# LSH attention and ternary feed-forward: a coarse column shift inside the score matmul, coefficients on GpSimd, two rounded passes for the ternary layers

## The chip, the core and the metric

The kernel runs on one core of a Trainium2 chip. The engines are TensorE (PE, with its weight loads PEld), VectorE (DVE), ScalarE (ACT), GpSimd (POOL) and the queue of SyncE (SP), which issues nearly all transfers. The metric is the device time of one execution in microseconds. Before the change it is 1344.95 us, the median of 3 runs (1344.68 to 1345.1).

## The reference

One layer on x of 16 images x 512 tokens x 128 features. First an attention of 16 heads with 8 features each, whose scores are q against q itself, then a feed-forward part with ternary weights; both read a layer norm of x and add a layer norm of their result to x.

```python
q = (x @ Wq.T + bq).reshape(B, S, H, Dh)
v = (x @ Wv.T + bv).reshape(B, S, H, Dh)
qa = jnp.concatenate([q, jnp.ones((B, S, H, 1), q.dtype)], axis=-1)
bits = (jnp.einsum('bshe,en->bshn', qa, hyperplanes) >= 0).astype(jnp.int32)
buckets = jnp.einsum('bshn,n->bsh', bits, 2 ** jnp.arange(NH, dtype=jnp.int32))
...
scores = jnp.einsum('bhsd,bhtd->bhst', q, q) / jnp.sqrt(jnp.float32(E))
same = (b_hs[:, :, :, None] == b_hs[:, :, None, :]).astype(scores.dtype)
coeff = NB - 2 + same                       # 62, or 63 in the same bucket of 64
attn = jax.nn.softmax(scores * coeff, axis=-1)
out = jnp.einsum('bhst,bhtd->bhsd', attn, v)
...
h = jax.nn.silu(_tlin(x, w1_w, w1_s)) * _tlin(x, w2_w, w2_s)     # 128 -> 512
h = jax.nn.gelu(_tlin(h, h1_w, h1_s), approximate=False)         # 512 -> 512
h = jax.nn.gelu(_tlin(h, h2_w, h2_s), approximate=False)         # 512 -> 512
return _tlin(h, w3_w, w3_s)                                      # 512 -> 128
```

`_tlin(x, w, s)` is x times the transposed w, scaled by s for each output; the entries of w are -1, 0 or 1.

## The kernel before, in words

The program is one long straight list of instructions for each engine. A small planner, the class `Order`, decides the order of that list while the program is built: every piece of work is a generator that asks for buffers from a `Pool`, waits on an `Event`, and yields one operation with an engine, a cost and a rank; the planner runs all generators against a simulated clock and emits an operation when its engine is free there. So the order on each engine is fixed before the program runs, and each engine works through it strictly in that order.

Index j counts the 256 heads of all images (j = 16 b + h), each with 4 tiles of 128 x 512.

- `prep(b)`, L605 to L807, makes q for image b, splits it into three bf16 parts (`qparts`), writes each part twice to memory (L651, L652), and makes the bucket numbers, once as rows (`bkd`) and once as columns (`bj`). `inputs()`, L533 to L600, finds mean and variance of x for the images after the first with accumulating activations on ScalarE.
- `gather(j)`, L812 to L853, fetches the parts of one head as two operands of 72 rows (9 products of parts, 8 features each) and the bucket row on 128 partitions. All three transfers go through SP.
- `scores()`, L872, makes one tile of scores in PSUM by one bf16 matmul. `coeffs()`, L890, makes the tile of coefficients 62 or 63 on VectorE. `logits()`, L925, multiplies both on VectorE and in the same instruction keeps the maximum of each row (the tile is symmetric, so the maximum of a row is that of a column too).
- `maxima()`, L958 and L963, turns the maxima of two heads and writes them to memory; `softmax()`, L975, reads them back as a row on all partitions (`mb`), subtracts that row from the four tiles on GpSimd in one instruction of 128 x 2048 (L982) and exponentiates on ScalarE (L987). Five heads (`BY_ROWS`) go another way, with the maximum as a bias.
- `attend(gg)`, L1048, multiplies the weights of four heads with v, four matmuls side by side in the array, with a column of ones that gives the denominators; L1069 turns the result, L1079 and L1080 divide.
- `residual`, `added` and `ffn(b)` follow for each image: gate products L1200 with w1 and w2, silu on ScalarE L1188, their product on VectorE L1170, two hidden layers L1244 with gelu L1258, the last layer L1282, norm and output. All these matmuls are float32. The last image runs in two halves. `weights()` loads the weights and folds scales and means into them.
- `activity()`, L1419, keeps TensorE busy with matmuls of zeros until the first feed-forward block starts.

Buffers that the change touches: 11 tiles of logits, 3 banks of PSUM for scores, 3 for the feed-forward part and 2 for the rest, 4 sets of gathered rows, 4 tiles of coefficients.

Of the kernel before, what the change touches and what calls it, by code (L numbers as in the profile page):

```python
# [14 lines left out]
BF16 = mybir.dt.bfloat16  # L15
AF = mybir.ActivationFunctionType
# [5 lines left out]
P = 128  # L22
EPS = 1e-5
NBKT = 64

# [165 lines left out]
def tile_lsh_attention_ffn(  # L191
    ctx: ExitStack,
    tc: tile.TileContext,
    x: bass.AP,
# [30 lines left out]
    KS = NP * NP * DH  # L225
    BR, BC, BP = 3, 172, 174
# [9 lines left out]
    LB = 11  # L236
    BY_ROWS = (3, 7, 11, 15, 19)
    SLOTS = H * NT
    N = B * SLOTS

# [39 lines left out]

    junk = const.tile([P, E], BF16, name="junk")
# [7 lines left out]

    block = const.tile([E, H], F32, name="block")  # L290
    nc.vector.reduce_sum(
        block, ident.rearrange("r (h d) -> r h d", d=DH), axis=AX.X
    )
    hp_sb = const.tile([E, H, NH], F32, name="hp_sb")
# [68 lines left out]
    score_banks = Pool("s", 3)  # L363
    ffn_banks = Pool("f", 3)
    banks = Pool("b", 2)
    logit_bufs = Pool("l", LB)
    row_bufs = Pool("r", 4)
    co_bufs = Pool("co", 4)
    mx_bufs = Pool("mx", 2)
    mb_bufs = Pool("mb", 3)  # L370
    row_mx_bufs = Pool("rx", 2)
    h_bufs = Pool("h", 3)
    x1_bufs = Pool("x1_", 2)
    xnt_bufs = Pool("xntf", 1)
    avs_bufs = Pool("avs", 1)
    a_bufs = Pool("a", 2)

    NB_ = B * NG
    gathered, exped = events(B * H), events(B * H)
    scored, weighed = events(N), events(N)  # L380
# [116 lines left out]
    def turned(xn, xnt, k, tp, tiles):  # L497

        cols = slice(tiles[0] * P, (tiles[-1] + 1) * P)

        def turn():
            for t in tiles:
                nc.tensor.transpose(tp[:, ts(t, P)], xn[:, t, :], ident)

        yield pe(0.125 * len(tiles), 2, turn)
        yield act(0.13 + 0.0925 * len(tiles), -2, lambda: nc.scalar.copy(xnt[:, cols], tp[:, cols]))
        od.put(banks, k)
# [21 lines left out]
    rs_x = const.tile([P, B, NT], F32, name="rs_x")  # L529
    nm_x = const.tile([P, B, NT], F32, name="nm_x")  # L530
    known = events(B)

    def inputs():  # L533
        for b0, b1 in zip(GROUPS, GROUPS[1:]):
            n = b1 - b0
            sums = const.tile([P, 2, n, NT], F32, name=f"sx_{b0}")
            ve = const.tile([P, n, NT], F32, name=f"vx_{b0}")
            late = 6 if b0 == 1 else LATE
            if b0 > 1:
                yield wait(gathered[1])  # L540
            for b in range(b0, b1):
                xt = p2.tile([P, NT, E], F32, tag="xtm", name=f"xtm_{b}", bufs=1)
                yield dma(
                    256,
                    2,
                    lambda: nc.sync.dma_start(
                        out=xt, in_=x[b].rearrange("(p t) e -> p t e", t=NT)
                    ),
                )

                def sum_(ts_):
                    for t in ts_:
                        nc.scalar.activation(
                            junk,
                            xt[:, t, :],
                            AF.Identity,
                            scale=ROOT / E,
                            accum_out=sums[:, 0, b - b0, t : t + 1],
                        )

                def square(ts_):
                    for t in ts_:
                        nc.scalar.activation(
                            junk,
                            xt[:, t, :],
                            AF.Square,
                            scale=-ROOT,
                            bias=sums[:, 0, b - b0, t : t + 1],
                            accum_out=sums[:, 1, b - b0, t : t + 1],
                        )  # L570

                yield act(1.0, late, lambda: sum_((0, 1)))
                yield act(1.0, late, lambda: sum_((2, 3)))
                yield act(1.2, late, lambda: square((0, 1)))
                yield act(1.2, late, lambda: square((2, 3)))
            yield act(
                0.22,
                -5,
                lambda: nc.scalar.activation(ve, sums[:, 1], AF.Identity, bias=eps),
            )  # L580
            yield pool(
                1.0,
                0,
                lambda: nc.gpsimd.tensor_tensor(
                    rs_x[:, b0:b1], ve, mhalf[:, 0:n], op=ALU.pow
                ),
            )
            k = yield get(banks)
            mp = bank(k, f"mp_{b0}")[:, 0 : n * NT].rearrange("p (b t) -> p b t", t=NT)
            yield act(0.22, -5, lambda: nc.scalar.copy(mp, sums[:, 0]))  # L590
            yield dve(
                0.1,
                1,
                lambda: nc.vector.scalar_tensor_tensor(
                    nm_x[:, b0:b1], mp, -(float(E) ** 0.5), rs_x[:, b0:b1], op0=ALU.mult, op1=ALU.mult
                ),
            )
            od.put(banks, k)
            for b in range(b0, b1):
                od.set(known[b])  # L600


    qds, bkds, bjs = {}, {}, {}

    def prep(b):  # L605
# [14 lines left out]
        if b:  # L620
            yield wait(known[b])
            xn = p2.tile([P, NT, E], F32, tag="xna", name=f"xn_a{b}", bufs=1)
            xnt = p1.tile([P, S], F32, tag="xnta", name=f"xnt_a{b}")
            yield from rescale(xt, lambda t: xn[:, t, :], (nm_x[:, b], rs_x[:, b]), ALL)
            k = yield get(banks)
            yield from turned(xn, xnt, k, bank(k, f"tp_a{b}"), ALL)
        else:
            xnt = p1.tile([P, S], F32, tag="xnta", name=f"xnt_a{b}")
            yield from norm_transposed(xt, xnt, f"a{b}", 1, ALL)
# [13 lines left out]
        qd = [  # L643
            dram.tile([H, DH, NP, S], BF16, tag="qd0", name=f"qd0_{b}"),
            dram.tile([H, NP, DH, S], BF16, tag="qd1", name=f"qd1_{b}"),
        ]
        kept = events(NP)

        def keep(i):
            def emit():  # L650
                nc.sync.dma_start(out=qd[0][:, :, i, :], in_=qparts[i])  # L651
                nc.sync.dma_start(out=qd[1][:, i, :, :], in_=qparts[i])  # L652

            yield dma(256, 1, emit, cost=0.7)
            od.set(kept[i])
# [97 lines left out]
        od.spawn(keep(0))  # L753
        yield wait(read)
# [57 lines left out]
    def gather(j, tag):  # L812
        b, h = divmod(j, H)
        yield wait(prepared[b])
        ql = p1.tile([KS, S], BF16, tag=f"ql{tag}", name=f"ql_{j}")
        qr = p1.tile([KS, S], BF16, tag=f"qr{tag}", name=f"qr_{j}")
        bb = p1.tile([P, BR * BP], BF16, tag=f"bb{tag}", name=f"bb_{j}")
        rows[j] = (ql, qr, bb, tag)

        yield dma(  # L820
            74,
            1 + j * 1e-3,
            lambda: nc.sync.dma_start(
                out=ql,
                in_=qds[b][1][h]
                .rearrange("i d s -> (i d) s")
                .unsqueeze(1)
                .to_broadcast([NP * DH, NP, S]),
            ),
            held=False,  # L830
# [658 lines left out]
```

## Time and profile before

| | |
|---|---|
| median of 3 runs | 1344.95 us |
| span of the profiled execution | 1343.1 us, granted TensorE clock 0.987 |
| transfers | 174.03 MB, mean 130 GB/s, 45.7% of 16 engines for the main queue |
| DVE L925, 1024 logit tiles with their maxima | 663.0 us busy, mean 678 ns |
| DVE L890, 1024 coefficient tiles | 450.1 us busy, mean 470 ns |
| ACT L987, 251 exponentials of a whole head | 478.2 us busy, mean 1908 ns |
| PE L1244, hidden layers, 1088 records for 544 matmuls | 495.5 us busy |
| PE L872, 1024 score matmuls | 346.6 us busy, mean 383 ns |
| PE L1048, weights times v, 2048 records for 1024 matmuls | 270.3 us busy |
| ACT table loads, 178 in all | 1283 ns each |

A group's line gives source line, engine, operation, output and inputs with their shapes, the count, then busy time and the mean duration of one, then the idle time just before these instructions and what ended it. Durations of neighbours overlap on an engine, since an instruction starts before the one in front of it has drained; so the groups' busy times add up to more than the engine's busy time, and the distance between two starts is the better price in a full queue. A float32 matmul shows as two records. In the timelines the columns are start, duration, engine, line, operation, tiles and count; in the table of stretches each engine's busy time and count are followed by the granted clock, the share of the transfer engines and their rate.

### The profile page before, as it was taken

Reading aid. Unit: us, or ns where it says so; the run is one execution under the profiler, and the core shown is the slowest. Engines: PE = TensorE matmul, PEld = TensorE weight load, DVE = VectorE, ACT = ScalarE, POOL = GpSimd, SP = SyncE. Lnnn points to the kernel's source line nnn. Section 1 sums busy time; section 2 is a strip of 40 time slices with the busy share of each in tenths; the row PEclk is TensorE's granted clock in tenths of the full one; section 3 lists DMA queues with packets and bytes.
Section 4 is the critical chain, followed back from the end, with each engine's and each line's share of the span. In section 5 each row is a group of like instructions: output and inputs, shape, how many; then the busy total and the mean of one; then the engine's idle time right before and its main releaser. Section 6 shows DMA issues by size and latency. Waiting matters only on the chain.

```text
span 1343.1 us, 21064 instructions
## 1 busy us (share of the span) xinstructions
PE 1293.6 (96%) x6009; PEld 577.7 (43%) x6009; DVE 1220.4 (91%) x3867; ACT 1119.6 (83%) x1560; POOL 1196.7 (89%) x316
## 2 busy tenths in 40 slices
PE   8999999998999999999999999999999999999897
PEld 3444344344443343444334344434444344434367
DVE  5999999999999899999999999999999999999220
ACT  3688888889998897988888788888989798888953
POOL 1497999999999999999999999999999999999810
PEclk9999999998999999999999999999999999999999
DMA  4755455455544445455544545454545545444100
GB/s 132 198 142 149 128 156 134 139 144 146 148 142 116 129 141 145 133 141 137 149 123 122 146 132 155 123 143 120 149 129 142 138 139 140 131 120 119 48 9 8
DMA packets 158865, 174.03 MB, mean 130 GB/s; under 512 B 33821, under 2 KB 117277, under 8 KB 158749
## 3 DMA queue, kind: packets, MB, share of 16 engines
q1 hardware_dynamic: 155937, 169.20, 45.7%
q10 hardware_dynamic: 2811, 3.48, 0.9%
q8 instruction: 48, 0.79, 0.2%
q14 instruction: 69, 0.56, 0.2%
HBM read 153.50 MB, written 19.13 MB: 129 GB/s over the span
## 4 chain that ended last, share of the span: by engine, by line
PE 55%; DVE 25%; DMA 7%; POOL 5%; issue 5%; ACT 3%; SPq 1%; POOLq 0%; ACTq 0%; DVEq 0%
PE hp L1244 23%; PE av L1048 12%; DVE l L925 12%; PE sp L872 10%; DVE co L890 9%; POOL l L982 5%; PE w L1200 4%; DMA mb<-md 4%; PE yp L1282 2%; PE op L1069 1%; DMA bb<-bkd 1%; DVE h L1170 1%; DMA ql<-qd 1%; ACT l L987 1%; PE pp L674 1%
## 5 line engine op out<-in xcount | busy, mean ns | idle before, releaser
L982 POOL TENSOR_TENSOR l<-l,mb 128x2048 f32<-128x2048 f32 x251 | 1134.9, 4553 | 39.8 <-DMA mb<-md 33.1
L925 DVE CUSTOM_DVE_ANT_0 l<-co,sp 128x512 f32<-128x512 bf16 x1024 | 663.0, 678 | 14.9 <-PE sp L872 10.0
L987 ACT ACTIVATE l<-l 128x2048 f32<-128x2048 f32 x251 | 478.2, 1908 | 38.9 <-POOL l L982 33.9
L1244 PE MATMUL hp<-h,h 128*128 128x512 f32 (+1 forms) x1088 | 495.5, 569 | 0.4 <-ACT h L1258 0.4
L890 DVE TENSOR_SCALAR co<-bb,bj 128x516 bf16<-128x516 bf16 x1024 | 450.1, 470 | 1.1 <-DMA bb<-bkd 0.7
L872 PE MATMUL sp<-qr,ql 72*128 72x512 bf16 x1024 | 346.6, 383 | 33.8 <-DVE mxpad L925 30.3
L1244 PEld LDWEIGHTS hp<-h,h 128*128 128x128 f32 x1088 | 202.0, 190 | 159.4 <-issue 134.7
L1048 PE MATMUL av<-l,vaug 128*32 128x512 f32 x2008 | 251.4, 607 | 0.0
L872 PEld LDWEIGHTS <-ql 72*128 72x128 bf16 x1024 | 91.2, 98 | 279.0 <-issue 258.4
L1200 PE MATMUL w<-xnt_f,w 128*128 128x512 f32 (+1 forms) x272 | 133.6, 591 | 4.4 <-ACT a L1188 4.2
L1048 PEld LDWEIGHTS av<-l,vaug 128*32 128x32 f32 x2008 | 55.1, 110 | 146.6 <-issue 123.2
L987 ACT ACT_TABLE_LOAD x87 | 111.6, 1283 | 1.5
L1419 PE MATMUL activity<-still 128*128 128x512 bf16 x325 | 89.5, 387 | 1.0 <-DVE still L283 1.0
L925 DVE DVE_READ_ACCUMULATOR2_ANT mxpad<- 128x1 f32 x1004 | 81.6, 81 | 0.0
L1258 ACT ACT_TABLE_LOAD x59 | 75.7, 1283 | 0.9
L1200 PEld LDWEIGHTS w<-xnt_f,w 128*128 128x128 f32 x272 | 51.5, 197 | 49.0 <-issue 23.8
L1062 ACT COPY avs<-av 128x512 f32<-128x512 f32 x64 | 37.0, 578 | 41.8 <-PE av L1048 41.6
L1170 DVE TENSOR_TENSOR h<-w,a 128x512 f32<-128x512 f32 (+1 forms) x68 | 44.1, 652 | 30.0 <-PE w L1200 19.6
L1282 PEld LDWEIGHTS yp<-w,h 128*128 128x128 f32 x512 | 65.4, 191 | 13.0 <-issue 9.0
L1282 PE MATMUL yp<-w,h 128*128 128x128 f32 x512 | 65.9, 275 | 0.0
L457 POOL TENSOR_TENSOR rs_y<-ve_y,mhalf 128x4 f32<-128x4 f32 (+1 forms) x17 | 16.5, 969 | 50.3 <-ACT ve_y L446 50.1
L1258 ACT ACTIVATE h<-hp,h1s 128x512 f32<-128x512 f32 (+1 forms) x68 | 42.0, 660 | 14.3 <-PE hp L1244 13.9
(105 smaller groups left out, 954.6 us busy)
## 6 DMA issues: line engine op xcount, KB each, us to landing
mb<-md SPq DMA_DIRECT2D x251, 256.0 KB
bb<-bkd SPq DMA_DIRECT2D x256, 130.5 KB
ql<-qd SPq DMA_DIRECT2D x256, 72.0 KB
qr<-qd SPq DMA_DIRECT2D x255, 72.0 KB
qd<-q SPq DMA_DIRECT2D x96, 128.0 KB
xta<-in_L_attn_x_dram SPq DMA_DIRECT2D x16, 256.0 KB
xtr<-in_L_attn_x_dram SPq DMA_DIRECT2D x16, 256.0 KB
xtm<-in_L_attn_x_dram SPq DMA_DIRECT2D x15, 256.0 KB
```

The lines of the kernel that those rows point to most:

```text
L872: nc.tensor.matmul(sp, lhsT=ql[:, ts(t, P)], rhs=qr, start=True, stop=True)
L890: nc.vector.tensor_scalar(co, bb.rearrange("p (r c) -> p r c", c=BP)[:, :, 0:BC], bjs[b][:, c : c + 1], float(NBKT - 2), op0=ALU.is_equal, ...
L925: nc.vector.tensor_tensor_reduce(out=l, in0=co[:, 0:S], in1=sp, scale=1.0, scalar=-3.0e38, op0=ALU.mult, op1=ALU.max, accum_out=mx[:, t : ...
L982: lambda: nc.gpsimd.tensor_tensor(l, l, mb.unsqueeze(1).to_broadcast([P, NT, S]), op=ALU.subtract),
L987: yield act(1.82, 0, lambda: nc.scalar.activation(l, l, AF.Exp, scale=SCALE), "exp")
L1048: nc.tensor.matmul(av[k * Q : (k + 1) * Q, :], lhsT=va[:, t, c : c + Q], rhs=ls[gg * GH + k][0][:, t, :], start=(t == 0), stop=(t == NT - 1),)
L1170: lambda: nc.vector.tensor_tensor(h[:, c, cols], g2, a, op=ALU.mult),
L1200: lambda: nc.tensor.matmul(gp, lhsT=w_sb[which][:, 0, ts(c, P)], rhs=xnt[:, cols], start=True, stop=True),
L1244: lambda i=i: nc.tensor.matmul(hp, lhsT=w[:, i, ts(c, P)], rhs=hin[:, i, cols], start=(i == 0), stop=(i == NC - 1),),
L1258: nc.scalar.activation(h[:, c, cols], hp, AF.Gelu, scale=sc[:, c : c + 1])
L1282: nc.tensor.matmul(yp[:, ts(t, E)], lhsT=h[:, i, ts(t, P)], rhs=w_sb["w3"][:, i, :], start=(i == 0), stop=(i == NC - 1),)
L1419: nc.tensor.matmul(bk, lhsT=still, rhs=still.unsqueeze(1).to_broadcast([P, NT, P]), start=start, stop=stop,)
```

## The change

- **The shift inside the score matmul.** For images 1 to 15 the maximum of a column is no longer found. Instead each query gets a level, its own squared length in steps, rounded and capped (`levels`). 64 rows are added to the score matmul's 64 rows of q: on one side the one-hot code of the bucket, on the other that code less 63, times the level (`code`). In the same bucket they add -62 x level, in another -63 x level; times the coefficient 63 or 62 both give the same number, so a whole column is shifted by a constant, which the softmax takes out again. One part product is dropped there (8 instead of 9). Exponentials then follow at once, with a fixed bias of -25 (`weights_of`). Image 0 keeps the old way, its subtraction cut in two.
- **q in memory** is now one chain of 10 slots for each head, of which an operand is slots 0 to 8 or 1 to 9, so that both operands come in one transfer (`qlr`).
- **Coefficients** of images 1 to 15 are made on GpSimd, and so is the one-hot code of each pair of heads; the second half of the code is made on VectorE, and SP writes it into the operand.
- **Two passes.** The inputs of w1, w2, h1 and h2 are split into a value rounded to float32r and the rest, and go through TensorE in two float32r passes; w3 stays float32. For the hidden layers GpSimd makes both (`split`). The scales no longer go into the weights, so the feed-forward norm subtracts its mean again.
- **silu** becomes tanh, times and plus on VectorE, with the scales in the product.
- **Moments of x** are taken in `prep` on VectorE; `inputs()` is gone.
- **A guard.** The new body notes whether all denominators lay within limits and whether all weights were unchanged by the rounding; at the end a branch on that number (`doubt`) runs the old form of the body in full if they did not.
- **Buffers.** 7 tiles of logits, 5 banks of PSUM shared by all but the scores, 6 sets of rows, 2 tiles of coefficients for image 0 and 6 for GpSimd's, 2 for codes of pairs, 2 for split halves.

```diff
+    CHAIN = (2, 2, 1, 1, 0, 1, 2, 0, 0, 2)
+    KS = (len(CHAIN) - 1) * DH
...
-        yield dma(74, ..., ql)
-        yield dma(74, ..., qr)
+                out=qlr[0:n],
+                in_=bass.AP(tensor=chain.tensor, offset=chain.offset + first * S,
+                    ap=[[S, n], [DH * S, 2], [1, S]]),
...
+        if b in running:
+            yield wait(coded[j])
+            code, i, kp, left = codes.pop(j)
+            yield dma(128, 1 + j * 1e-3,
+                lambda: nc.sync.dma_start(
+                    out=qlr[NBKT:P], in_=code[i * NBKT : (i + 1) * NBKT]), cost=0.43)
...
-                    nc.vector.tensor_scalar(
+                    (nc.gpsimd if pooled else nc.vector).tensor_scalar(
                         co,
                         bb.rearrange("p (r c) -> p r c", c=BP)[:, :, 0:BC],
                         bjs[b][:, c : c + 1],
                         float(NBKT - 2),
                         op0=ALU.is_equal,
                         op1=ALU.add,
                     )
...
+                    if mx is None:
+                        nc.vector.tensor_tensor(l[:, t, :], co, sp, op=ALU.mult)
+                        return
...
+    def weights_of(j, l):
+        yield act(1.82, 0, lambda: nc.scalar.activation(
+            l, l, AF.Exp, bias=base, scale=SCALE), "exp")
+        od.set(exped[j])
...
+    def levels(b, square):
+        yield pe(0.3, 2, lambda: nc.tensor.matmul(rowp, lhsT=own, rhs=square, start=True, stop=True))
+        yield dve(0.6, 2, lambda: nc.vector.tensor_scalar(
+            rowp, rowp, LEVELS, WHOLE, op0=ALU.min, op1=ALU.add))
+        yield dve(0.6, 2, lambda: nc.vector.tensor_scalar(
+            level, rowp, -WHOLE, UNIT, op0=ALU.add, op1=ALU.mult))
...
+    def code(b, h, kp):
+        yield dma(132, ..., pb, in_=bkds[b][two].unsqueeze(1).to_broadcast([2, NBKT, BR * BP]))
+        yield dma(128, ..., pz, in_=zds[b][two].unsqueeze(1).to_broadcast([2, NBKT, S]))
+        yield pool(0.55, RHOT, mark)            # hot[:, 0] = (pb == number)
+        yield dve(0.6, RCODE, lambda: nc.vector.scalar_tensor_tensor(
+            hot[:, 1, :], hot[:, 0, :], 1.0 - NBKT, pz, op0=ALU.add, op1=ALU.mult))
...
+                nc.scalar.activation(a, gp, AF.Tanh, scale=w_sb["w1sh"][:, c : c + 1])
+                nc.vector.scalar_tensor_tensor(a, a, 1.0, gp, op0=ALU.add, op1=ALU.mult)
...
+                nc.vector.scalar_tensor_tensor(
+                    h[:, c, cols], g2, w_sb["gs"][:, c : c + 1], a, op0=ALU.mult, op1=ALU.mult)
...
+        def split(layer, hin, khin, before):
+                    yield pool(..., nc.gpsimd.tensor_copy(hi[:, :, cols], hin[:, two, cols]))
+                yield pool(..., nc.gpsimd.tensor_tensor(
+                    lo[:, :, cols], hin[:, two, cols], hi[:, :, cols].bitcast(F32), op=ALU.subtract))
...
+                for k, r in enumerate(rs):
+                    nc.tensor.matmul(hp, lhsT=w[:, i, ts(c, P)], rhs=r,
+                        start=(i == 0 and k == 0), stop=(i == NC - 1 and k == len(rs) - 1))
...
+def tile_lsh_attention_ffn(tc, *args):
+    with tc.tile_pool(name="verdict", bufs=1) as kept:
+        doubt = kept.tile([1, 1], I32, name="doubt")
+        body(tc, doubt, *args)
+        v = nc.values_load(doubt, min_val=0, max_val=2**20)
+    with tc.If(v > 0):
+        body(tc, None, *args)
```

## The prediction

> **What bounds the kernel now.** I read the page's busy shares first, then the stretches, the groups and the timelines of single engines.
>
> ```profile
> span 1343.1 us, 21064 instructions
> PE 1293.6 (96%) x6009; PEld 577.7 (43%) x6009; DVE 1220.4 (91%) x3867; ACT 1119.6 (83%) x1560; POOL 1196.7 (89%) x316
> ```
>
> ```profile
> core 0: us, PE busy (x) PEld busy (x) DVE busy (x) ACT busy (x) POOL busy (x), PEclk, DMA share, GB/s
> 0.00:60.00 60.00, 56.07 (x250) 25.92 (x251) 43.38 (x141) 27.75 (x73) 19.01 (x15) 1.00 0.56 157
> 60.00:600.00 540.00, 520.18 (x2469) 224.20 (x2468) 525.51 (x1660) 476.35 (x726) 513.34 (x127) 0.98 0.51 141
> 600.00:1240.00 640.00, 625.79 (x2887) 269.19 (x2889) 631.53 (x2004) 554.95 (x649) 629.00 (x161) 0.99 0.49 135
> 1247.00:1343.10 96.10, 84.86 (x374) 54.87 (x374) 13.08 (x43) 55.35 (x102) 28.39 (x13) 0.97 0.06 20
> ```
>
> From 60 to 1240 us VectorE and GpSimd both stand at 97 to 98%: two full engines in one ring. The last 96 us belong to the last feed-forward blocks on TensorE. The groups say what fills them:
>
> ```profile
> L982 POOL TENSOR_TENSOR l<-l,mb 128x2048 f32<-128x2048 f32 x251 | 1134.9, 4553 | 39.8 <-DMA mb<-md 33.1 <-DVE co L890 5.2 <-DVE mxpad L925 1.5
> ...
> L1362 POOL TENSOR_TENSOR w<-w,scale 128x512 f32<-128x512 f32 x2 | 2.5, 1268 | 15.3 <-DMA scale<-in_L_ffn_w_s_dram 15.3
> ...
> masks.py:199 POOL TENSOR_SCALAR_AFFINE_SELECT ident<-ident 128x128 f32<-128x128 f32 x1 | 0.3, 295 | 0.0
> ...
> L987 ACT ACT_TABLE_LOAD x87 | 111.6, 1283 | 1.5
> ```
>
> Means overlap in a full queue, so I price by distance from start to start.
>
> ```profile
> 700.31 0.68 DVE L925 CUSTOM_DVE_ANT_0 l<-co,sp 128x512 f32<-128x512 bf16 x1
> 700.92 0.08 DVE L925 DVE_READ_ACCUMULATOR2_ANT mxpad<- 128x1 f32 x1
> 700.92 0.86 DVE L890 TENSOR_SCALAR co<-bb,bj 128x516 bf16<-128x516 bf16 x2
> 701.70 0.67 DVE L925 CUSTOM_DVE_ANT_0 l<-co,sp 128x512 f32<-128x512 bf16 x1
> ...
> 713.14 0.69 DVE L1170 TENSOR_TENSOR h<-w,a 128x512 f32<-128x512 f32 x1
> 713.75 0.47 DVE L890 TENSOR_SCALAR co<-bb,bj 128x516 bf16<-128x516 bf16 x1
> ```
>
> ```profile
> 841.69 0.61 PE L872 MATMUL sp<-qr,ql 72*128 72x512 bf16 x2
> 842.13 1.02 PE L1244 MATMUL hp<-h,h 128*128 128x512 f32 x2
> 842.99 0.60 PE L1069 MATMUL op<-ident,avs 128*128 128x128 f32 x4
> ```
>
> So a logit (L925) costs VectorE 0.605 us, a coefficient (L890) 0.39, a plain product from PSUM (L1170) 0.61. TensorE takes 0.22 us for 512 bf16 columns and 0.86 for a float32 matmul, which is two records. Eight subtractions in a row took 36.11 us, 4.51 each.
>
> **VectorE, term by term.** Before: 1024 x (0.605 + 0.39) = 1019, 127 transposes of the maxima 17 (0.13 each), rest 1220 - 1036 = 184. After:
> - 960 logits as plain products, by L1170: 960 x 0.605 = 581. Leaving out the maximum gains nothing, since both rows cost the same. Image 0 keeps the old form: 64 x 0.995 = 64.
> - 120 codes, one per two heads (L1086). Lower end the coefficient's 0.39, upper end 0.67, the distance 13.20 to 13.87 of the scalar_tensor_tensor L758; it is that operation, so 0.67: 80 (47 to 80).
> - The gate of tanh (L1376): 60 x 0.67 + 8 x 0.42 = 44; the product becomes three-operand: 60 x 0.06 = 4.
> - xnt's low part 15 x 0.61 + 2 x 0.42 = 10; levels 30 x 0.67 = 20; moments of x, which ScalarE made before (statistics 64 x 0.22, aggregates 64 x 0.09, scale 60 x 0.13): 28; the means now needed for the feed-forward input: 8; the bound on the denominators, 120 x 0.17 = 20; comparing the weights with their rounded form, 4 passes of 2048 elements and 4 of 512: 12.
>
> Sum 581 + 64 + 226 + 184 = 1055, which is 165 less than before (1010 at the low ends).
>
> **GpSimd.** Removed: 251 - 12 subtractions, 239 x 4.51 = 1078. The 12 left are cut in halves, 24 x 2.36 = 57. By L982 and L1362 a two-input operation costs 0.17 + 2.14 us per 1000 elements: (4553 - 1268) / 1536. Added: 64 subtractions of the halves of h, 60 x 2.36 + 8 x 1.27 = 152. Everything with one input has only the 295 ns row: (295 - 173) / 128 = 0.95 ns an element, so 0.66 us for 512, less the 0.04 by which a subtraction's mean exceeds its distance: 0.62. Its ends are 0.42 (bf16 at half the bytes, 0.17 + 512 x 0.48) and 1.27 (as dear as two inputs, L1362). I take 0.62: the affine select is the one row with one input. 960 coefficients and 120 marks: 1080 x 0.62 = 670. Copies of halves 60 x 1.15 + 8 x 0.66 = 74; powers 64; weights 7. Sum 670 + 57 + 152 + 74 + 64 + 7 = 1024 (808 to 1726).
>
> Here a rule speaks against the change: the Trainium skill, GPSIMD Engine Reference, section "4.1 Engine selection", says that elementwise work belongs on VectorE because GpSimd is about twice as slow, though one-input work is roughly line-rate. Twice this case's 0.39 would be 0.78 a coefficient, GpSimd 1196 us and the whole about 1315; line rate would leave VectorE the bound. A second one, SBUF — State Buffer, section "Who interferes with whom", says that a VectorE operation with two SBUF inputs locks out a GpSimd operation that reads SBUF. By it the 120 codes could cost GpSimd 80 us more and the whole about 1220. No row before shows either.
>
> **TensorE.** Before, by distances: scores 1024 x 0.22 = 225, L1244 480 x 0.86 + 64 x 0.43 = 440, L1200 110, av 128 x 1.86 = 238, yp 57, op 28, the small rest 68: 1166, and start-up filler. The price of a rounded float32 pass isn't in the trace; its ends are 0.22 and 0.86. A bf16 matmul streams 512 columns once in 0.22; 0.86 is four streams, as for two halves by two halves; a rounded operand has one half. So 0.22: L1244 960 x 0.22 + 128 x 0.11 = 225, L1200 57, levels 3, the score's 128 rows no dearer than 72 (columns set it): 901. At 0.43 a pass nothing is gained; at 0.86 TensorE would hold 1720.
>
> **ScalarE** loses 65 us of sums over x (L553, L563 with their accumulator reads) and 74 of 178 table loads, 95 us, since tanh asks for no load of its own; it gains 15 squares, 10. About 965, off the bound.
>
> **Transfers and waits.** The 256 KB broadcast of maxima goes for 239 heads. In its place: nine or ten copies of q per image for six, two broadcasts per pair of heads, and one 128 KB write of the code per head: 169 MB for 174. SP's queue has some 1250 issues for 1330. The code's write (L860) waits on SP for VectorE's code; behind it stand the next heads' rows, x and the output. Two pair buffers cover it: load 3.2 us (like mb), mark 0.62 behind at most one 2.4 us subtraction, code 0.67, write 3.2, some 10 us of the 16 that two pairs have. Without the cover each us over is 120 us at most. GpSimd's coefficients now stand in one queue with the splits: 3.5 us of split is covered by six coefficient buffers, 6 x 0.605 = 3.6. The logit buffers fall from 11 to 7, but the subtraction's 4.5 us stay and its broadcast's 3 fall out: priced at 0 to 40 us, taken 8.
>
> **The sum.** VectorE's idle time before was 17 us in the first 60, 23 to 1240, and 83 in the tail. The tail loses the pile of subtractions (some 13 us) and half of the matmuls (440 + 110 over 16 images is 34 an image, half of that for the last two), and gains the splits on GpSimd, 14 + 15, partly in the chain: some 70 us, 20 of them VectorE's, so 50 idle. 1055 + 17 + 23 + 50 + 8 = 1153; the branch at the end and the 2 us by which the median of the runs (1344.95) exceeds the span: **1155**. GpSimd the same way: 1024 + 41 at the front + 38 + 37 in the tail = 1140, just below.
>
> **Rivals.**
> - *GpSimd becomes the bound, still faster.* Every 0.1 us on the one-input price is 108 us. From 0.64 it decides; 0.74 gives 354 + 799 + 116 + 2 = 1271. A late code, or a logit buffer missing, ends in the same place, some 1200 to 1300. For: GpSimd is full now and gets 1080 more instructions. Against: nothing but one 295 ns row.
> - *Slower by the comparison on GpSimd.* From 0.81 us an instruction the sum passes 1345; at L1362's 1.27 it is 354 + 1372 + 118 = 1844. For: a comparison isn't in the trace at all, and 512 elements have cost 1.27 there.
> - *Rounded passes not cheaper.* At 0.43, TensorE keeps 1176 us and a longer tail: about 1290. At 0.86 about 1850.
> - *The fallback runs.* Then the old program follows the new, about 2500. Worked out from the inputs, the shifted denominators lie between 6e-21 and 5e12, inside the limits 1e-26 and 1e34, and all weights are -1, 0, 1.
>
> **Chances.** VectorE-bound, 1090 to 1200: 0.61. GpSimd-bound or starved but faster: 0.20. Passes at 0.43: 0.05. Slower by the comparison 0.09, by dear passes or the fallback 0.04, no change 0.01. The likeliest gives 1155. Low end: VectorE at 1010 and a 60 us tail, 1090; the high end goes into the second case to 1270. Faster by over 0.2% 0.86, within 0.2% (about what this measurement can tell from none) 0.01, slower 0.13.
>
> **What would show it.** After: one-input GpSimd rows of 0.58 to 0.66; VectorE near 1055 and over 95% in the middle; L1505 at 0.22 from start to start; some 104 table loads; a tail of 70 us. Wrong if VectorE waits on GpSimd's coefficients or for the code's write, or if GpSimd's row for 128x512 is over 0.7.

## The result, and the profile after: GpSimd is the bound at twice the time

The changed kernel takes 2578.6 us (median of 4 runs, 2577.29 to 2579.45) against 1345.03 us (4 runs, 1344.68 to 1347.29): a ratio of 1.917 with a 95% interval of 1.914 to 1.920. The forecast of 1155 us, and its range to 1270, were wrong. The fallback did not run: the page counts 20872 instructions, fewer than the 21064 of before, which alone would be one old body.

The head of the page, and the table of stretches (after the stretch and its length come PE, PEld, DVE, ACT and POOL, busy time and count each, then the granted clock, the transfers' share and GB/s):

```profile
span 2576.4 us, 20872 instructions
PE 1468.1 (57%) x6082; PEld 685.4 (27%) x6082; DVE 1202.3 (47%) x2440; ACT 1024.6 (40%) x1260; POOL 2444.0 (95%) x1326
```

```profile
core 0: us, PE busy (x) PEld busy (x) DVE busy (x) ACT busy (x) POOL busy (x), PEclk, DMA share, GB/s
...
600.00:1240.00 640.00, 354.48 (x1385) 162.79 (x1384) 287.18 (x571) 259.88 (x318) 635.95 (x342) 0.70 0.26 66
1240.00:2400.00 1160.00, 627.86 (x2540) 290.36 (x2539) 528.90 (x1029) 467.11 (x549) 1149.33 (x615) 0.72 0.26 65
```

Two engines at 97 to 98% have become one at 99% (635.95 of 640, 1149.33 of 1160). VectorE, forecast to be over 95% busy, stands at 45 to 46%, and the granted clock has fallen to 0.70 and 0.72 with TensorE busy for 54 to 55% of these stretches. The groups of the page, with the two that GpSimd got and the VectorE work behind them:

```profile
L914 POOL TENSOR_SCALAR co<-bb,bj 128x512 bf16<-128x512 bf16 x960 | 1908.5, 2019 | 14.2 <-DVE l L962 13.5
L962 DVE TENSOR_TENSOR l<-co,sp 128x512 f32<-128x512 bf16 x960 | 634.3, 682 | 717.2 <-POOL co L914 647.6
...
L1086 DVE SCALAR_TENSOR_TENSOR hot<-hot,pz 128x512 bf16<-128x512 bf16 x120 | 167.9, 1401 | 485.1 <-POOL hot L1074 481.3
...
L1074 POOL TENSOR_SCALAR hot<-pb,number 128x512 bf16<-128x512 bf16 x120 | 192.9, 1611 | 0.0
L1462 POOL TENSOR_TENSOR h<-h,h 128x1024 fp32r<-128x1024 f32 (+1 forms) x68 | 153.8, 2264 | 1.4
...
L1457 POOL CAST h<-h 128x1024 fp32r<-128x1024 f32 (+1 forms) x68 | 68.4, 1010 | 21.0 <-PE hp L1505 14.9
```

960 coefficients at 2.02 us are 1908.5 of GpSimd's 2444.0 us. GpSimd's subtractions (L1462) and copies (L1457), 154 and 68 us, stand where the forecast put them. What waits for that, from the list of waits (total, times, longest), and GpSimd's queue in the middle of the run, from its timeline:

```profile
ACT l L1007 <- DVE l L962: 685.3, 151, 14.1
DVE l L962 <- POOL co L914: 647.6, 419, 6.5
DVE hot L1086 <- POOL hot L1074: 481.3, 104, 10.4
```

```profile
1493.48 13.85 POOL L914 TENSOR_SCALAR co<-bb,bj 128x512 bf16<-128x512 bf16 x7
1507.29 1.58 POOL L1074 TENSOR_SCALAR hot<-pb,number 128x512 bf16<-128x512 bf16 x1
```

Seven coefficients without a gap take 13.85 us, 1.98 from start to start, where the sum had 0.62; the mark has 1.58. VectorE's products wait 419 times for a coefficient and ScalarE's exponentials for the products. The wait of L1086 is for the mark, which stands in the same full queue. Two of the signs of being wrong that the prediction had named are here: a GpSimd row over 0.7 us, and VectorE waiting for GpSimd's coefficients.

### The profile page after: what moved, and what is told of

It is laid out like the page before. It is cut to its first block, busy times and chain, and to the rows that moved or that the text cites. A ratio compares the mean times of both kernels' runs of the same rounds, so it can differ in the third digit from the quotient of the medians.

```text
span 2576.4 us, 20872 instructions
## 1 busy us (share of the span) xinstructions
PE 1468.1 (57%) x6082; PEld 685.4 (27%) x6082; DVE 1202.3 (47%) x2440; ACT 1024.6 (40%) x1260; POOL 2444.0 (95%) x1326
## 5 line engine op out<-in xcount | busy, mean ns | idle before, releaser
L914 POOL TENSOR_SCALAR co<-bb,bj 128x512 bf16<-128x512 bf16 x960 | 1908.5, 2019 | 14.2 <-DVE l L962 13.5
L962 DVE TENSOR_TENSOR l<-co,sp 128x512 f32<-128x512 bf16 x960 | 634.3, 682 | 717.2 <-POOL co L914 647.6
L888 PE MATMUL sp<-qlr 128*128 128x512 bf16 (+1 forms) x1024 | 467.8, 482 | 841.7 <-DVE l L962 796.7
L1007 ACT ACTIVATE l<-l,base 128x2048 f32<-128x2048 f32 x240 | 480.3, 2002 | 686.4 <-DVE l L962 685.3
L1086 DVE SCALAR_TENSOR_TENSOR hot<-hot,pz 128x512 bf16<-128x512 bf16 x120 | 167.9, 1401 | 485.1 <-POOL hot L1074 481.3
L1199 PE MATMUL av<-l,vaug 128*32 128x512 f32 x2016 | 332.8, 781 | 34.0 <-DVE h L1376 9.6
L888 PEld LDWEIGHTS <-qlr 128*128 128x128 bf16 (+1 forms) x1024 | 103.5, 109 | 759.0 <-issue 713.9
L1074 POOL TENSOR_SCALAR hot<-pb,number 128x512 bf16<-128x512 bf16 x120 | 192.9, 1611 | 0.0
L1462 POOL TENSOR_TENSOR h<-h,h 128x1024 fp32r<-128x1024 f32 (+1 forms) x68 | 153.8, 2264 | 1.4
L1457 POOL CAST h<-h 128x1024 fp32r<-128x1024 f32 (+1 forms) x68 | 68.4, 1010 | 21.0 <-PE hp L1505 14.9
```

Of the source, the lines that this page charges most:

```text
L888: nc.tensor.matmul(sp, lhsT=qlr[:, 0, ts(t, P)], rhs=qlr[:, 1, :], start=True, stop=True,)
L914: (nc.gpsimd if pooled else nc.vector).tensor_scalar(co, bb.rearrange("p (r c) -> p r c", c=BP)[:, :, 0:BC], bjs[b][:, c : c + 1], float(N ...
L962: nc.vector.tensor_tensor(l[:, t, :], co, sp, op=ALU.mult)
L1007: 1.82, 0, lambda: nc.scalar.activation(l, l, AF.Exp, bias=base, scale=SCALE), "exp"
L1074: (nc.gpsimd if HOT == "pool" else nc.vector).tensor_scalar(hot[:, 0, :].rearrange("p (r c) -> p r c", c=BC), pb.rearrange("p (r c) -> p r ...
L1086: lambda: nc.vector.scalar_tensor_tensor(hot[:, 1, :], hot[:, 0, :], 1.0 - NBKT, pz, op0=ALU.add, op1=ALU.mult),
```

## The experiments

### What a GpSimd instruction costs, by itself

Two kernels leave the attention and the feed-forward work out and issue six of each form in a row, on 512 columns. The edit is a list of this kind:

```diff
+ gpsimd.tensor_scalar(cb, rows(bb), col, 62.0, op0=is_equal, op1=add)        # L54
+ gpsimd.tensor_scalar(cb, rows(bb), col, None, op0=is_equal)                 # L56
+ gpsimd.tensor_scalar(cb, bb[:, 0:512], 5.0, 62.0, op0=is_equal, op1=add)    # L60
+ gpsimd.tensor_scalar(cb, bb[:, 0:512], 0.0, 62.0, op0=mult, op1=add)        # L62
+ gpsimd.tensor_scalar(cb, bb[:, 0:512], col, None, op0=mult)                 # L64
+ gpsimd.tensor_copy(cb, bb[:, 0:512])                                        # L74
```

> A kernel that computes nothing of the reference (its output is zeros): it runs GpSimd's instruction forms one after the other, first alone, then beside streams of VectorE instructions. Theory A (the comparison is dear): the form of the coefficient alone takes about 2.0 us, with multiply in place of the comparison at most 0.7. Theory B (the bf16 type is dear): bf16 forms take about 2.0 whatever the operation, float32 forms 0.6 to 0.7. Theory C (the row pattern or the scalar read through a pointer): contiguous input or an immediate brings it to 0.7. Theory D (VectorE takes the SBUF port): alone the coefficient takes 0.6 to 0.7, and about 2.0 only beside VectorE. Under A to C the time doesn't change beside VectorE's product from PSUM.

The groups of that kernel; L98 is L54 once more, beside scalar_tensor_tensor operations with two SBUF inputs on VectorE:

```profile
L98 POOL TENSOR_SCALAR cb<-bb,col 128x512 bf16<-128x512 bf16 x6 | 14.8, 2460 | 0.7 <-DVE cd L94 0.2
...
L54 POOL TENSOR_SCALAR cb<-bb,col 128x512 bf16<-128x512 bf16 x6 | 12.0, 2000 | 2.6 <-DVE col L41 2.2
...
L60 POOL TENSOR_SCALAR cb<-bb 128x512 bf16<-128x512 bf16 x6 | 11.5, 1922 | 0.5
L64 POOL TENSOR_SCALAR cb<-bb,col 128x512 bf16<-128x512 bf16 x6 | 9.4, 1566 | 0.6
L56 POOL TENSOR_SCALAR cb<-bb,col 128x512 bf16<-128x512 bf16 x6 | 9.4, 1564 | 0.6
...
L62 POOL TENSOR_SCALAR cb<-bb 128x512 bf16<-128x512 bf16 x6 | 3.7, 620 | 0.5
L74 POOL COPY cb<-bb 128x512 bf16<-128x512 bf16 x6 | 3.7, 615 | 0.3
```

The coefficient is 2.00 us by itself, so it is no matter of neighbours, waits or order. Type and pattern make no difference (1.997 to 2.000 over five forms). But multiply and add by two immediates take 0.62, and so does a copy. That left two candidates for what makes the others dear, the comparison or the scalar read from SBUF, and a second list parted them:

```diff
+ gpsimd.tensor_scalar(cb, bb[:, 0:512], 5.0, None, op0=is_equal)             # L54
+ gpsimd.tensor_scalar(cb, bb[:, 0:512], 5.0, None, op0=mult)                 # L56
+ gpsimd.tensor_scalar(cb, bb[:, 0:512], col, 62.0, op0=mult, op1=add)        # L58
+ gpsimd.tensor_scalar(cb, bb[:, 0:512], 5.0, 62.0, op0=max, op1=add)         # L62
+ gpsimd.tensor_scalar(cb, bb[:, 0:512], 5.0, 62.0, op0=is_ge, op1=add)       # L66
+ gpsimd.tensor_scalar(cb, bb[:, 0:512], 5.0, None, op0=max)                  # L70
+ gpsimd.tensor_scalar(cb[:, 0:256], bb[:, 0:256], col, 62.0, op0=is_equal, op1=add)   # L74
+ gpsimd.tensor_scalar(hr, hf, col, 62.0, op0=is_equal, op1=add)              # L76, 1024 columns
+ gpsimd.affine_select(out=cf, in_=bf[:, 0:512], ...)                         # L78
```

> The attention and feed-forward work is left out; outputs are zeros. More cells of GpSimd's tensor_scalar with 512 bf16 columns, alone on the chip. Known so far: multiply and add by two immediates 0.62 us, a copy 0.615, is_equal with a per-partition scalar 1.56, with an add behind it 2.00, is_equal and add by immediates 1.92, multiply by a per-partition scalar 1.57. Theory A (each of the two, a comparison or a scalar read from SBUF, leaves the fast form by itself): is_equal by an immediate alone some 1.5, is_ge the same, multiply by a per-partition scalar then add 2.0, add by a per-partition scalar 1.57, max and subtract by immediates 0.62. Rival B (the time goes by the number of operations outside one fast pair, multiply then add): everything but multiply and add is slow, max and subtract too, at 1.5 for one operation and 1.9 for two. The 128 x 512 affine select should take 0.66 as the 128 x 128 one of 0.295 was scaled up in the prediction. 256 columns of the coefficient: 1.0 if it goes by the element, 1024 columns 3.9.

```profile
L76 POOL TENSOR_SCALAR hr<-hf,col 128x1024 f32<-128x1024 f32 x6 | 22.4, 3726 | 0.5
...
L66 POOL TENSOR_SCALAR cb<-bb 128x512 bf16<-128x512 bf16 x6 | 11.5, 1923 | 0.5
L62 POOL TENSOR_SCALAR cb<-bb 128x512 bf16<-128x512 bf16 x6 | 11.5, 1921 | 0.5
...
L56 POOL TENSOR_SCALAR cb<-bb 128x512 bf16<-128x512 bf16 x6 | 8.9, 1491 | 0.5
L54 POOL TENSOR_SCALAR cb<-bb 128x512 bf16<-128x512 bf16 x6 | 8.9, 1489 | 1.5 <-DVE bb L38 1.1
...
L74 POOL TENSOR_SCALAR cb<-bb,col 128x256 bf16<-128x256 bf16 x6 | 6.9, 1145 | 0.6
L58 POOL TENSOR_SCALAR cb<-bb,col 128x512 bf16<-128x512 bf16 x6 | 4.2, 695 | 0.6
L78 POOL TENSOR_SCALAR_AFFINE_SELECT cf<-bf 128x512 f32<-128x512 f32 x6 | 3.7, 614 | 0.3
```

The first theory misses, and the rival holds, with both its sizes (1.5 and 1.9). The scalar from SBUF is not the cause: with multiply then add it costs 0.695, some 0.075 more than an immediate. Nor is it the comparison alone: one multiply by an immediate, with nothing behind it, takes 1.49 as is_equal and max do, and two operations other than multiply then add take 1.92. Of the forms tried, only the pair multiply then add, the copy and the affine select run at 0.62; any other single operation is 1.49, any other pair 1.92, plus 0.075 for a scalar from SBUF. The coefficient grows with its columns (1.145, 2.000, 3.726 us for 256, 512, 1024). The affine select at 512 is 0.614, so the forecast's scaling of its row was right, and its use for a tensor_scalar wrong.

### The same coefficients back on VectorE

```diff
-HEADS_C = tuple(range(16))
+HEADS_C = ()          # coefficients of all heads on VectorE
-NCO = 2
+NCO = 6
-HOT = "pool"          # in the second of the two runs
+HOT = "dve"           # the marks too
```

> The coefficients of all heads go back to VectorE (six buffers for them), all else as in the changed kernel. If GpSimd's coefficients make the 2578 us: GpSimd then holds 354 + 120 x 1.6 = 546 us, VectorE 1055 + 960 x 0.39 = 1429, and the whole is 1429 + 100 = 1500 to 1560. With VectorE's coefficients at the 0.30 that image 0 shows undisturbed it would be 1420 to 1480. If something else held the 2578 (the code's transfers, seven logit buffers, the slower TensorE clock), it stays above 1800.

> As before, and the one-hot marks go to VectorE too. GpSimd 354 us, VectorE 1429 + 120 x 0.39 = 1476. If VectorE's code instruction took 1.40 us rather than 0.67 because GpSimd held the port, it should fall to 0.67 to 0.75 here, 80 us less, and the whole is within 40 us of the run with marks on GpSimd. If the 1.40 has another cause it stays.

1728.1 and 1713.5 us: taking the 2 us instructions off GpSimd gives 850 us back, but less than expected. What was expected of the code instruction (L1086) came: with the marks on VectorE too its mean is 0.695 us, for 1.40 in the changed kernel. The page of the second, with its chain of waits:

```profile
PE 1261.8 (74%) x6098; PEld 607.0 (35%) x6098; DVE 1461.7 (85%) x3520; ACT 1028.9 (60%) x1268; POOL 364.1 (21%) x246
...
DVE 29%; DMA 29%; PE 28%; issue 8%; SPq 4%; ACT 2%; POOL 1%; DVEq 0%; POOLq 0%
DMA pz<-zd 24%; PE av L1199 10%; DVE l L962 9%; DVE co L914 8%; PE sp L888 7%; PE hp L1505 6%; DVE hot L1086 2%; DVE h L1351 2%; PE activity L1835 2%; PE yp L1601 1%; SPq L1058 1%; DMA qlr<-qd 1%; DVE h L1376 1%; DMA bb<-bkd 1%; PE w L1392 1%
```

VectorE's work is what the sum says (1461.7), but 250 us of idle time come on top, where the forecast had 98, and the transfer of pz holds 24% of the chain. So there was a second error, hidden behind the first. Were two pair buffers too few? A run with three (`NPB = 3`, and `NCO = 4`) asks that:

> Coefficients and marks all on VectorE as in the run of 1713.5 us, but three pair buffers for codes instead of two, and 4 coefficient buffers for 6. Theory A (the chain of the code, two broadcasts, mark, code, write, does not fit into two pair buffers): the idle share of VectorE falls from 15% to some 5%, time 1540 to 1600. Rival B (the idle time comes from elsewhere, the scores' order or SP's queue): 1690 to 1740, unchanged.

1700.7 us, VectorE 86% busy: the second theory held. A third pair buffer did not remove the idle time; what it is worth by itself this run does not show, since it has two coefficient buffers fewer as well.

### GpSimd's price set to what the forecast assumed

```diff
-                        bjs[b][:, c : c + 1],
+                        0.0 if pooled else bjs[b][:, c : c + 1],
                         float(NBKT - 2),
-                        op0=ALU.is_equal,
+                        op0=ALU.mult if pooled else ALU.is_equal,
                         op1=ALU.add,
...
-HOT = "pool"
+HOT = "dve"
```

> The coefficients of images 1 to 15 stay on GpSimd, but as multiply by 0 and add 62, both immediates: the comparison of buckets is left out of them, every coefficient is 62. The one-hot mark is made on VectorE. Price of such an instruction alone: 0.62, 0.69 from start to start. Theory A (the price of the comparison on GpSimd is the whole miss; with the price that the prediction assumed, its sum holds): GpSimd 364 + 960 x 0.69 = 1026, VectorE 1462 - 960 x 0.39 = 1088, time 1190 to 1270. Rival B (the ring of code transfers, marks and buffers that left VectorE idle for 250 us in the run with all of it on VectorE binds by itself): 1340 to 1700, VectorE under 80% busy, with waits on transfers of pz, pb and on the code's write at the head.

1558.8 us, VectorE 75% busy: the rival held. The price went to 0.63 us, GpSimd to 935.4 us or 60%, and the time fell by 1020 us. But the kernel is still 400 us from the forecast, and some 210 us slower than the kernel before: with GpSimd's price as assumed, the forecast would have been wrong even so. VectorE's waits in that run, and a piece of its chain of waits (start, duration, what):

```profile
DVE hot L1086 <- DMA pz<-zd: 170.0, 92, 3.9
...
DVE hot L1074 <- DMA pb<-bkd: 31.9, 25, 3.2
```

```profile
717.80 11.90 DMA pz<-zd
...
729.79 0.70 DVE hot L1086
...
730.51 0.46 SPq L860
```

The transfer of pz is issued at 717.80 and lands 11.90 us later; the code (L1086) starts at once, and then its write (L860) goes out, for which SP has waited, with all other transfers behind it in SP's queue. On the chain, the 57 landings of pz among its longest pieces take 10.4 us on average (the next expectation has 58 and 10.3, one too many), and 6 of pb 9.0. The forecast had 3.2, read from the row broadcast of mb in the kernel before. The bucket row bb, a broadcast of as many bytes, took 4.7 on this chain, the mean of four.

### One row for each transfer

pz and pb carry two heads, each row repeated 64 times. The edit asks for the same bytes in two transfers:

```diff
-                out=pz, in_=zds[b][two].unsqueeze(1).to_broadcast([2, NBKT, S])
+        for i in range(2):
+                out=pz[i * NBKT : (i + 1) * NBKT],
+                in_=zds[b][h + i].partition_broadcast(NBKT),
...
```

The same is done for pb. First on the run before, with the comparison left out, then with three pair buffers:

> As the run of 1558.8 us (coefficients on GpSimd as multiply and add by immediates, the comparison left out, marks on VectorE), but the two broadcasts of a pair, pb and pz, each go as two transfers of one head's row to 64 partitions, in place of one transfer with a pattern of 2 rows x 64 repeats. In that run pz took 8.6 to 14 us from issue to landing (mean 10.3 over 58 on the chain that ended last), while the broadcast of one row to 128 partitions (bb), as many bytes, took 3 to 5. Theory A (the two-row pattern is spread over few of the transfer engines, and this slow landing is the ring that kept VectorE idle): pz lands in 3 to 5 us, the waits on pz and pb fall from 202 us to under 60, time 1250 to 1400. Rival B (pz waits in the queue behind bursts of other transfers that SP releases late): it lands in 8 to 12 us as before, time 1500 to 1600, a little more for 240 more issues on SP.

> As the run with row transfers and the comparison left out, with three pair buffers in place of two and five coefficient buffers in place of six. If the number of pair buffers mattered beside the slow landing, this is 30 us or more faster than the same with two; if the landing alone was the ring, both agree within 15 us.

1371.3 and 1331.5 us. The first theory held: pz lands in 2.7 us (the median) and the waits for pz and pb, 202 us before, are gone from the head of the list, whose longest is now the one for scores:

```profile
DVE l L962 <- PE sp L888: 49.0, 54, 2.5
```

With the landing mended, the third pair buffer (with five coefficient buffers for six) is worth another 40 us, where in the run of 1700.7 it and fewer coefficient buffers were worth 13. In the second run the other terms of the sum can be read, since neither error is in it (page; stretches with the columns as above; groups):

```profile
PE 1150.8 (87%) x6082; PEld 576.3 (43%) x6082; DVE 1158.7 (87%) x2560; ACT 1016.8 (76%) x1266; POOL 954.5 (72%) x1206
```

```profile
0.00:60.00 60.00, 51.06 (x221) 23.03 (x222) 45.25 (x140) 19.27 (x35) 21.38 (x26) 0.97 0.60 159
60.00:1200.00 1140.00, 995.46 (x5271) 484.56 (x5270) 1053.50 (x2267) 920.22 (x1094) 860.45 (x1099) 0.94 0.52 137
1200.00:1329.60 129.60, 104.29 (x593) 68.72 (x592) 59.98 (x155) 77.36 (x139) 72.65 (x83) 0.91 0.16 41
```

```profile
L1091 DVE SCALAR_TENSOR_TENSOR hot<-hot,pz 128x512 bf16<-128x512 bf16 x120 | 98.6, 822 | 0.5
L1079 DVE TENSOR_SCALAR hot<-pb,number 128x512 bf16<-128x512 bf16 x120 | 63.6, 530 | 0.3 <-DMA pb<-bkd 0.3
L1257 DVE SCALAR_TENSOR_TENSOR sound<-rd,sound 128x16 f32<-128x16 f32 x120 | 56.2, 468 | 2.1
```

Whether the second error matters for the changed kernel itself was asked with that edit alone, nothing else changed:

> The changed kernel in full, with the two broadcasts of a pair as two transfers of one row each; nothing else. Theory A (GpSimd's coefficients are the first bound, the landing of pz the second, hidden behind it): 2540 to 2590, unchanged within 1.5%, GpSimd 95% busy. Rival B (both lie on one chain and add): 2350 to 2450, below the sum that GpSimd now shows plus its front and tail, some 2530.

2575.5 us against 2578.6, GpSimd 95% busy: nothing. While GpSimd needs 2 us for a coefficient, the late code is hidden behind it. The two causes are in a row, not side by side.

### Why the two-row transfer lands late

Alone on the chip, attention and feed-forward left out, each transfer followed by a copy on VectorE that waits for it:

```diff
+ sync.dma_start(out=cb, in_=rd[0].partition_broadcast(P))                    # L56
+ sync.dma_start(out=cb, in_=rd[0:2].unsqueeze(1).to_broadcast([2, 64, 512])) # L59
+ ... [4, 32, 512], [8, 16, 512], two transfers of 64, [1, 64, 512]           # L62, L65, L71, L75
```

> The attention and feed-forward work is left out; outputs are zeros. One SP queue, nothing else on the chip: a transfer from memory into 128 partitions x 1 KB, a copy of it on VectorE, and the next transfer, six times each, so that the distance between copies is issue, landing and copy. Patterns: one row to 128 partitions; 2 rows x 64 repeats (that of pz); 4 x 32; 8 x 16; 16 x 8; two transfers of one row to 64 partitions each; one row written as 1 x 64 repeats to 64 partitions. Theory A (a transfer is shared out among the engines by the rows of its outer dimension): one row to 128 some 3 us; 2 x 64 9 to 10; 4 x 32 5 to 7; 8 x 16 4 to 5; 16 x 8 3; two of 64 about 3.5; 1 x 64 9 to 10. Rival B (the slow landing came from other transfers in front of it): all 128-partition patterns within 20% of one another at 3 us.

One copy of each from VectorE's timeline (in brackets what it waited for): one row to 128 partitions, 2 x 64, 4 x 32, 8 x 16, and two transfers of one row:

```profile
18.14 0.29 DVE L57 COPY cd<-cb 128x512 bf16<-128x512 bf16 x1 [2.96 <-DMA cb<-rd]
...
40.03 0.29 DVE L60 COPY cd<-cb 128x512 bf16<-128x512 bf16 x1 [4.65 <-DMA cb<-rd]
...
66.20 0.29 DVE L63 COPY cd<-cb 128x512 bf16<-128x512 bf16 x1 [3.41 <-DMA cb<-rd]
...
83.98 0.29 DVE L66 COPY cd<-cb 128x512 bf16<-128x512 bf16 x1 [2.88 <-DMA cb<-rd]
...
123.75 0.29 DVE L73 COPY cd<-cb 128x512 bf16<-128x512 bf16 x1 [3.27 <-DMA cb<-rd]
```

The order is the one that sharing by rows would give: the wait is 4.65 for two rows, 3.41 for four, 2.88 for eight, and 2.5 for sixteen. But the sizes are smaller than expected, and 1 x 64 took 2.6 only. Alone, the pattern explains 1.7 of the 7 us by which pz's 10.4 exceed the forecast's 3.2. A last kernel put such transfers behind one another:

> The attention and feed-forward work is left out; outputs are zeros. One SP queue; each block is done four times, and a copy on VectorE waits for its last transfer. Alone, 2 rows x 64 repeats took 5.0 us from copy to copy and one row to 128 partitions 3.25. Theory A (the two-row pattern uses few transfer engines, so such transfers queue behind one another while others pass): eight of them in a row 20 us or more from copy to copy, eight of one row to 128 partitions 7 to 8 (issue-bound at some 0.6 each); two in a row 7 to 8; two behind three ordinary ones 9 to 10, as in the kernel; two pairs of single rows behind three ordinary ones 5.5 to 6.5. Rival B (only a longer fixed delay, no queue): eight in a row 9 to 10, two 5.6, two behind three ordinary ones 7.5.

Eight two-row transfers in a row, eight of one row to 128 partitions, two two-row ones behind three ordinary ones, and two pairs of single rows behind three ordinary ones:

```profile
75.48 0.29 DVE L59 COPY cd<-ring 128x512 bf16<-128x512 bf16 x1 [23.20 <-DMA ring<-rd]
...
141.16 0.29 DVE L63 COPY cd<-ring 128x512 bf16<-128x512 bf16 x1 [13.16 <-DMA ring<-rd]
...
203.91 0.29 DVE L73 COPY cd<-ring 128x512 bf16<-128x512 bf16 x1 [7.96 <-DMA ring<-rd]
...
231.26 0.29 DVE L80 COPY cd<-ring 128x512 bf16<-128x512 bf16 x1 [6.94 <-DMA ring<-rd]
```

Eight take 23.5 us from copy to copy against 13.4, so each adds 2.9 us where the ordinary one adds 1.7 (not the 0.9 of the expectation); two by themselves take 5.9, below the 7 to 8 expected; behind three others, two of them take 8.3 to 8.9 after the first round, the single rows 6.4 to 7.7. The two-row pattern is dear in a queue, which speaks for the first theory. The share of the transfer engines on this kernel's page, in tenths over 40 slices of 6.3 us, speaks for it too:

```profile
DMA  0111111111111115687776421111223218454398
```

The ones at the front are the two-row transfers, the digits up to 8 behind them the ordinary ones. From 10 to 85 us the share is 0.14 of 16 engines, the work of 2.2 of them, at 45 GB/s; from 105 to 140 us it is 0.76, that of 12, at 77 GB/s. So transfers of two rows, even eight in a row, keep about two engines busy. The kernel of 1558.8 us shows the same share, 0.14 from 739.5 to 742.8 us, at the end of a landing of pz that took 9.34. How the kernel's 10.4 us are made up, and why 1 x 64 is not slow, stays open; that two transfers of one row mend it is shown.

### A version that computes everything

GpSimd at 2 us and VectorE at 0.39 can share the coefficients:

```diff
-HEADS_C = tuple(range(16))
+HEADS_C = (1, 3, 5, 8, 10, 12, 14)
-HOT = "pool"
+HOT = "dve"
-                    yield pool(0.55, RCO, emit) if pooled else dve(0.39, 4, emit)
+                    yield pool(2.05, RCO, emit) if pooled else dve(0.39, 4, emit)
```

> Coefficients of 7 heads in 16 on GpSimd, the others and the marks on VectorE, with the planner told 2.05 us for GpSimd's; three pair buffers, 3 and 4 coefficient buffers. By the prices measured: GpSimd 364 + 420 x 2.07 = 1233, VectorE 1462 - 420 x 0.39 = 1298. Theory A (the two engines' sums decide, the code chain fits): 1380 to 1460. Rival B (the ring binds): 1500 to 1700, VectorE under 85%.

> The whole computation: coefficients of 7 heads in 16 on GpSimd (planned at 2.05 us), the rest and the marks on VectorE, as in the run of 1599.0 us, with the broadcasts of a pair as two transfers of one row each, two pair buffers, 3 and 6 coefficient buffers. Theory A (landing of pz and pb was the ring): VectorE's sum of about 1300 and some 100 idle, 1390 to 1460; still slower than before, since GpSimd's sum of 1210 and VectorE's 1300 both lie at or over what they were. Rival B (the ring is elsewhere): 1560 to 1620.

1599.0 us, and 1559.3 with transfers of one row: the first theory misses both times. The second run also has two pair buffers for three and six coefficient buffers for four, so the 40 us between them are not the transfers' alone. In it GpSimd's sum is right (1217.8 for 1233). VectorE holds 1364.5 for 1298, and its coefficients are the row that is too long, 325.4 us where 604 x 0.39 would be 236:

```profile
L914 DVE TENSOR_SCALAR co<-bb,bj 128x512 bf16<-128x512 bf16 x604 | 325.4, 570 | 0.1
```

Half of them take 0.35 us or less, but single ones up to 2.58; of what they take over 0.35, some 78 us lie beside two-input subtractions on GpSimd and some 42 beside its coefficients (more on this in the last section). And 193 us of idle time remain, 88 of them between 60 and 1380 us (1232.3 busy of 1320), 90 behind that. The longest wait in it is that for scores, 51.7 us; what would shorten it was not tried. No version that makes every coefficient came below the kernel before. With all coefficients of images 1 to 15 at 0.65 us on GpSimd, the comparison left out, and three pair buffers, the time was 1331.5 beside 1345.5 for the kernel before: one run of each, 1% apart.

## Why the prediction was wrong, point by point

- **The step that failed: "Everything with one input has only the 295 ns row ... 0.62. Its ends are 0.42 ... and 1.27".** The term 1080 x 0.62 = 670 measured 960 x 1.98 + 120 x 1.58 = 2090. Put into the forecast's own sum, GpSimd has 354 + 2090 = 2444, which is what the page shows (2444.0), and with its idle time (41 + 38 + 37) and 2 the sum gives 2562, within 1% of 2578.6. So the structure of that sum was right and one price was wrong by a factor of 3.2. The upper end was no bound: a two-input subtraction at 1.27 does not bound a one-input comparison at 2.00. The text itself said that a comparison was nowhere in the trace, and then gave the case that hung on it 9 in 100.
- **The rival "slower by the comparison on GpSimd"** had the right instruction and the right engine; its price of 1.27 and so its 1844 us were too low. It is not the comparison alone, since a single multiply takes 1.49. And its point of decision, 0.81 us, did not come out: at 0.63 us, with the marks on VectorE, the kernel took 1558.8 us and was still slower than before.
- **"Two pair buffers cover it: load 3.2 us (like mb)"** failed too. The two-row broadcast lands in 10.4 us in the kernel. It costs nothing while GpSimd is the bound, and 188 us (1558.8 to 1371.3) once it isn't. The prediction had put a late code at some 1200 to 1300; the run of 1558.8 us is that case.
- **VectorE 1055** was 5% low where it can be compared: logits 0.605 from start to start, codes alone 0.69. In the changed kernel it is 1202.3, with 88 more for the codes (1.40 each for 0.67). In the 1331.5 us run, which has the marks on VectorE (47 more, so 1102), it is 1158.7: the bound on denominators measured 56 for 20, the codes 99 for 80, the marks 64 for 47; the groups' means hold some waiting.
- **Idle time** of 98 in the sum is 171 there: 15 in the first 60 us, 86 up to 1200, 70 in the tail of 130 us, for 17, 31 and 50. So even with both errors mended the forecast was 176 us low.
- **What held:** GpSimd's other terms (copies 68 for 74, subtractions 154 for 152; 954.5 measured in the 1331.5 us run, where 1024 less 74 for the marks is 950); table loads (104 of 104); a rounded pass at 0.24 for 0.22 where the queue was full (28 passes in 6.64 us near the end of the changed kernel), so the rival of dear passes fell; the guard stayed silent. ScalarE was 60 us too low (1025 for 965), off the bound.
- **The rules of the Trainium skill that the prediction weighed.** GPSIMD Engine Reference, "4.1 Engine selection": its factor of two is for two-input operations; for one input, which is what a coefficient has, it says roughly line-rate. The row shows 2.00, five times VectorE's 0.39, and only multiply-add, copies and the affine select, at 0.61 to 0.62, came near the rule. SBUF — State Buffer, "Who interferes with whom", has such VectorE operations contend with GpSimd's reads, and this is shown: a coefficient on GpSimd took 2.46 for 2.00 beside VectorE operations of the code's form, and of these one at each GpSimd instruction took 1.06 for 0.69. In the changed kernel this is small for GpSimd, 2.02 for 2.00, some 18 us over 960, where the prediction had up to 80. For VectorE's codes it is larger, 1.40 us.

## What to carry to other kernels

An engine's price belongs to one operation with its operands: an operation that the trace does not show has no price there, and a neighbouring row, two-input or not, is no upper bound for it; issue six of it on the chip before 1000 are moved. Put the break-even price beside the unknown one (here 0.81 us by the forecast's sum, and lower in fact, since 0.63 us still gave a slower kernel), and when that many instructions hang on it, let the chances follow. When the first cause is mended, look again: a second one, here the landing of a broadcast of two rows, may have been hidden behind it.

## What the runs showed of the hardware that was not expected

- GpSimd's tensor_scalar with 512 columns is 0.62 us for multiply then add, but 1.49 for a multiply alone: one operation less is 2.4 times dearer.
- VectorE's coefficient of 512 columns (353 ns alone) is held for the whole of a GpSimd subtraction of two SBUF inputs. Beside four subtractions, which kept their 4.50 us, four coefficients took 4.54 to 4.57 us each, and the 36 after them 0.35 again; the group's mean, 773 ns, hides this. Beside GpSimd's comparison single ones took up to 0.74. The product from PSUM stays at 687.
- The kernel before ran 956 of its 1024 coefficients beside such subtractions, and none took over 0.49 us. It laid a coefficient tile out as three rows of 172 columns, the changed kernel as four rows of 128, which takes 0.35 alone but up to 2.57 in the run with all coefficients on VectorE. That the layout makes the difference was not tried.
- A broadcast of 128 KB as 2 rows x 64 repeats takes 5.0 us from copy to copy alone, that of one row 3.25, and 2.9 for 1.7 each in a queue of eight, with the work of some 2 and some 12 of the 16 transfer engines.
